# Layer 1's diagonal blocks in ten of 16 tiles, six turned on VectorE, and a quarter of the moves on ACT's queue

## The chip, the cores and the metric

The kernel runs on one core of a Trainium2 chip. A core has four compute engines that matter here: TensorE (PE, matmuls and 128x128 transposes), VectorE (DVE), ScalarE (ACT) and GpSimd (POOL). SyncE (SP) computes nothing and issues DMAs; ACT and POOL can issue them as well. Each engine runs its own list of instructions in order, and engines wait for one another on semaphores. Operands lie in the on-chip memory SBUF (128 partitions); matmuls write to PSUM. The metric is the device time of the core in microseconds, as a median over runs.

## The reference, cut to what matters

The input x is (4, 128, 64, 64): four batches, C = 128 channels, N = 4096 tokens. Everything is f32. Two layers follow one another, then a recurrent scan:

```python
# layer 0: group norm, then attention with q and k of 64 channels, gated, projected, residual
x = x + conv_attention(group_norm(x))
# layer 1
t = tokens(x)                                   # (4, 4096, 128)
h = layer_norm(t)
q = einsum('bsd,de->bse', h, W)
scores = einsum('bsd,btd->bst', q, q)           # symmetric in s and t
t = t + einsum('bst,btd->bsd', softmax(scores), h)
# FFN: batch norm over all tokens, then a scan over the 4096 tokens of each batch
wx = batch_norm(layer_norm(t) @ Wf.T)
y_t = sigmoid(wx_t + y_{t-1} @ V.T)
t = t + y
```

The point for this change is layer 1: its queries are also its keys, so the matrix of scores is symmetric, and so is its elementwise exponential. The tile for (queries s, keys t) is the transpose of the tile for (queries t, keys s).

## The kernel before, in words

**Tiling.** Of each batch, layer 1 takes the 4096 tokens as NB = 8 blocks of QB = 512 columns, and each block as NQ = 4 tiles of P = 128. A block pair (n, a) means the 512 queries of block n against the 512 keys of block a: 16 tiles of 128x128. The loop at the end of `layer1` runs over n in the order 6, 7, 5, 4, 3, 2, 1, 0 and, within each, over a from n down to 0 (`order`; the last batch's n = 0 is the exception). Because of the symmetry only pairs with a <= n are computed: one pair serves block n's output with its tiles as they are, and block a's output with its tiles turned.

**A pair takes two steps, i = 0 and i = 1.** In each, TensorE computes the scores of two key tiles against 512 queries into one of two PSUM buffers `ps` (line 726), ACT takes their exponential into `e`, one of four buffers (L730), and, if `turns(n, a)` holds (a < n, except for the last batch's pair (1, 0)), VectorE transposes the 32x32 squares of `e` into `dd`, one of two buffers (line 733). Transposing within 32x32 squares leaves the squares in the wrong partitions. So after the second step SP issues 16 DMAs of 64 KB each, from 32 partitions of `dd` to 32 partitions of `tt`, one of three buffers (lines 758 to 763, the DMA itself L760). They stay within SBUF.

**The products.** `direct` (lines 602 to 611) multiplies `e` by h of block a into the PSUM tile `o` of block n, two matmuls over 512 columns for each step, two steps later (LAG). `reversed_products` (lines 613 to 623) multiplies the turned tiles in `tt` by h of block n for block a, four matmuls, when the step count `clock` has gone on by 4 since the moves were issued. VectorE adds the finished `o` into `oacc` (`part`). When a block has all its parts, `finish` loads its tokens `t` with an SP DMA (line 655) and puts `tokens`, `turn` and `inputs` on the list `pending`, from which each step takes one. They normalize the block, write the turned result with four SP DMAs (line 279), and compute the FFN's input `wx`, which SP writes out (line 697). If `pending` is empty, a step takes a piece from `ahead`, the next batch's layer-0 inputs.

**The diagonal pair (a = n)** is not turned into `dd`. Its step i = 0 is like any other: scores over 2 x 512 columns. Its step i = 1 is `quarter` (lines 573 to 592): two matmuls over 256 columns for the lower right quarter (L578), four 128x128 transposes on TensorE that turn two tiles of each of the two key tiles of the first step's `e` (L584), an exp over 512 columns and a copy of 512 columns on ACT (L588 and L592). The products of a diagonal pair are the four 512-column matmuls of `direct`.

**Order.** At the start of the program the order of instructions is written by hand; after that (line 797) the framework's scheduler lays out each engine's list from the program as written, and the tile pools decide which buffer each allocation gets. In the built program every DMA of a queue signals one of eight completion counters, taken in turn, so that an issue waits until the DMA eight before it has landed. Layer 0 (line 461), the loads of the next batch's x, and, just before the last batch's layer 1, three SP loads of 2 MB each for `wxs` (line 820, the FFN's inputs of the batches already done) stand on the same SP queue as layer 1's moves.

## Time and profile before

| what | value |
|---|---|
| median of 3 runs | 3046.68 us (3046.57 to 3047.66) |
| the profiled execution's own time | 3047.56 us |
| its span in the trace | 3045.7 us |
| granted TensorE clock, mean | 0.994 |
| layer 1, as it stands in the trace | four stretches, one for each batch, of some 365 to 400 us |
| VectorE's transposes of squares (L733), 128x512 | 281.7 us in x444, 682 ns mean |
| exp of a step of layer 1 (L730), 128x1024 | 1.11 us mean, x258 |
| scores of layer 1 (L726), 128x512 | 482.9 us in x1032 records |
| direct products (L605), 128x512 | 537.0 us in x1160 records |

The page gives busy times of each engine, the span in 40 slices, the DMA queues, the chain of work that ended last, and groups of instructions by line, operation and shape. Two things are needed to read it. A matmul's record overlaps the one after it, because matmuls are pipelined, so the mean of a group is not the time at which the next one can begin; the pitch between successive ones is read from the chain in order of time. And an f32 matmul stands as two records, so counts of matmul records are twice the counts in the code (transposes have one).

The engines' rows in the 40 slices show where layer 1 lies: in its slices VectorE stands at 3 to 5 tenths, against 6 elsewhere, and 85 GB/s and more are moved, while TensorE stands at 9 in nearly all slices of the span.

### The profile page before, as it was taken

The numbers are of one execution on the slowest core, as the hardware profiler recorded it, in microseconds if no ns is written. First come the engines' busy times: TensorE is split into PE (matmuls) and PEld (weight loads), VectorE is DVE, ScalarE is ACT, GpSimd is POOL, SyncE is SP. The second block draws the span as 40 slices with busy tenths as digits, with TensorE's granted clock in tenths as the row PEclk, the third lists the DMA queues.
The fourth block names the chain that finished last, engine by engine and source line by source line (L and its number), as shares of the span: only waits on it lengthen the run. The fifth ranks groups of instructions, "written<-read, shape, count | busy, mean of one in ns | idle before, by whom it ended". The sixth has DMA issues, their size and how long they took to land.

```text
span 3045.7 us, 31528 instructions
## 1 busy us (share of the span) xinstructions
PE 2989.5 (98%) x10720; PEld 1371.1 (45%) x10720; DVE 1677.2 (55%) x3114; ACT 1032.2 (34%) x1151; POOL 221.0 (7%) x215
## 2 busy tenths in 40 slices
PE   9999999999999999999999999999999999999985
PEld 4444444444444444444444444444444444444442
DVE  6666654434666664444466665443456666333356
ACT  3444432222344432222244443222234443222224
POOL 0011100000011110000011101000001111000000
PEclk9999999999999999999999999999999999999998
DMA  1112143434122123333311114343422113544333
GB/s 42 41 53 56 52 117 87 97 90 99 41 56 56 48 85 96 94 96 87 87 46 56 42 47 118 85 98 87 101 58 59 39 49 90 143 100 102 96 119 151
DMA packets 246986, 241.09 MB, mean 79 GB/s; under 512 B 90016, under 2 KB 162208, under 8 KB 245792
## 3 DMA queue, kind: packets, MB, share of 16 engines
q1 hardware_dynamic: 246816, 238.98, 29.6%
q8 instruction: 88, 1.44, 0.2%
q14 instruction: 82, 0.67, 0.1%
HBM read 65.80 MB, written 56.62 MB: 40 GB/s over the span
## 4 chain that ended last, share of the span: by engine, by line
PE 92%; DVE 3%; SPq 2%; ACT 1%; DMA 0%; issue 0%; POOL 0%; DVEq 0%; POOLq 0%; ACTq 0%
PE o L476 28%; PE o L605 15%; PE ps L238 14%; PE ps L726 14%; PE ot L618 12%; SPq L760 2%; PE m L267 1%; PE m L689 1%; PE mp L438 1%; PE ps L578 1%; PE mq L570 1%; PE mp L369 1%; PE mp L423 1%; DVE t2s L900 1%; DVE ps_r L873 1%; PE m L680 1%
## 5 line engine op out<-in xcount | busy, mean ns | idle before, releaser
L476 PE MATMUL o<-e,nxt 64*128 64x512 f32 x4096 | 973.1, 589 | 0.0
L240 ACT ACTIVATE e<-ps 128x1024 f32<-128x1024 f32 x512 | 520.9, 1023 | 687.1 <-PE ps L238 648.1
L247 DVE TENSOR_TENSOR acc<-acc,e 128x1024 f32<-128x1024 f32 x448 | 547.6, 1222 | 228.5 <-ACT e L240 212.4
L476 PEld LDWEIGHTS o<-e,nxt 64*128 64x128 f32 x4096 | 403.4, 187 | 482.9 <-issue 474.1
L238 PE MATMUL ps<-nxt 64*128 64x512 f32 x2048 | 541.6, 595 | 1.9 <-ACT e L592 0.8
L605 PE MATMUL o<-e,h 128*128 128x512 f32 x1160 | 537.0, 592 | 0.0
L730 ACT ACTIVATE e<-ps,shift 128x1024 f32<-128x1024 f32 x258 | 287.2, 1113 | 646.3 <-PE ps L726 357.9
L726 PE MATMUL ps<-qt 128*128 128x512 f32 x1032 | 482.9, 594 | 2.7 <-ACT qt L571 2.7
L618 PE MATMUL ot<-tt,h 128*128 128x512 f32 x888 | 400.9, 593 | 0.0
L733 DVE STREAM_TRANSPOSE dd<-e 128x512 f32<-128x512 f32 x444 | 281.7, 682 | 137.9 <-ACT e L730 83.7
L605 PEld LDWEIGHTS o<-e,h 128*128 128x128 f32 x1160 | 218.8, 190 | 268.2 <-issue 268.0
L238 PEld LDWEIGHTS ps<-nxt 64*128 64x128 f32 x2048 | 197.9, 187 | 231.0 <-issue 148.8
L726 PEld LDWEIGHTS ps<-qt 128*128 128x128 f32 x1032 | 189.9, 190 | 219.3 <-issue 190.8
L618 PEld LDWEIGHTS ot<-tt,h 128*128 128x128 f32 x888 | 167.8, 190 | 210.2 <-issue 205.3
L627 DVE TENSOR_TENSOR oacc<-oacc,ot 128x512 f32<-128x512 f32 x87 | 59.7, 687 | 288.4 <-PE ot L618 288.4
L145 POOL TENSOR_SCALAR rstd<-mv 128x4 f32<-128x4 f32 x64 | 14.5, 226 | 2374.9 <-DVE mv L300 2374.9
L532 DVE SCALAR_TENSOR_TENSOR t<-yt,rinv,t 128x128 f32<-128x128 f32 x128 | 36.5, 347 | 80.2 <-DMA yt<-turn_d 80.2
L493 POOL TENSOR_SCALAR xb<-xb,bpc 128x512 f32<-128x512 f32 x32 | 61.6, 1924 | 243.9 <-DMA xb<-in_x_dram 234.3
L543 POOL TENSOR_SCALAR h<-h 128x512 f32<-128x512 f32 x32 | 72.3, 2261 | 63.7 <-DVE d L275 61.7
L588 ACT ACTIVATE e<-ps,shift 128x512 f32<-128x512 f32 x32 | 22.0, 687 | 144.1 <-PE ps L584 133.8
L146 POOL TENSOR_TENSOR rstd<-rstd,mhalf 128x4 f32<-128x4 f32 x64 | 66.4, 1037 | 5.3
L629 DVE COPY oacc<-ot 128x512 f32<-128x512 f32 x24 | 16.6, 691 | 85.6 <-PE ot L618 85.5
(156 smaller groups left out, 1611.2 us busy)
## 6 DMA issues: line engine op xcount, KB each, us to landing
tt<-dd SPq DMA_DIRECT2D x1776, 64.0 KB, 2.0
turn_d<-d SPq DMA_DIRECT2D x384, 64.0 KB, 1.8
nxt<-in_x_dram SPq DMA_DIRECT2D x16, 512.0 KB, 5.6
xb<-in_x_dram SPq DMA_DIRECT2D x32, 256.0 KB, 3.3
t<-turn_d SPq DMA_DIRECT2D x32, 256.0 KB, 2.7
yt<-turn_d SPq DMA_DIRECT2D x32, 256.0 KB, 2.7
t_d<-t SPq DMA_DIRECT2D x32, 256.0 KB, 2.0
qt<-turn_d SPq DMA_DIRECT2D x32, 256.0 KB, 2.9
```

Source lines behind the costliest of these rows:

```text
L146: nc.gpsimd.tensor_tensor(dst, dst, mhalf[:, :n], ALU.pow)
L238: nc.tensor.matmul(ps[:, h, :], lhsT=lhsT, rhs=rhs, start=True, stop=True)
L240: nc.scalar.activation(e, ps, AF.Exp, scale=scale)
L247: nc.vector.tensor_tensor(acc, acc, e, ALU.add)
L476: nc.tensor.matmul(o[r], lhsT=v[rs, p + h * PAIRS, :], rhs=e[rs, h, :], start=(p == 0 and h == 0), stop=(p == PAIRS - 1 and h == 1),)
L493: biased = nc.gpsimd.tensor_scalar(xb, xb, bpc, None, ALU.add)
L543: nc.gpsimd.tensor_scalar(hn, hn, 1.0, None, ALU.add)
L605: nc.tensor.matmul(o, lhsT=h[:, NQ * a + 2 * i + half, :], rhs=e[:, half, :], start=(a == order(n)[0] and i == 0 and half == 0), stop=(a = ...
L618: nc.tensor.matmul(ot, lhsT=h[:, NQ * n + j, :], rhs=t[:, :, j, :, :].rearrange("q p k j -> q k p j"), start=(j == 0), stop=(j == NQ - 1),)
L726: nc.tensor.matmul(ps[:, half, :], lhsT=qt[:, bass.ts(at, P)], rhs=qt[:, bass.ts(n, QB)], start=True, stop=True,)
L730: nc.scalar.activation(e, ps, AF.Exp, bias=shift)
L733: nc.vector.transpose(d.rearrange("q f b k j -> q k b f j")[:, 2 * i + half], e[:, half, :].rearrange("q (b f j) -> q b f j", b=NQ, f=NQ),)
```

## The change

A new function `upper(n, a)` holds for the diagonal pair of blocks n = 2 to 7, which is six pairs in each batch and 24 in all. For them only the tiles on and above the diagonal are computed, ten of 16: the scores of key tile j cover the columns from j x 128 on. In step i = 0 these are 512 and 384 columns, packed into 896 columns of `ps` and `e`; in step i = 1 256 and 128, packed into 384. Exp runs over the packed columns. `direct` multiplies just these columns.

The six tiles above the diagonal are turned by VectorE (`turn_tiles`, three transposes of 128, 256 and 256 columns in step 0, one of 128 in step 1) into a packed `dd` and moved to `tt` by 16 DMAs of 24 KB. `own_products` multiplies them into the same `o` with three matmuls over 384, 256 and 128 columns, due three steps after the moves are issued. `quarter` stays for the diagonal pairs of n = 1 and n = 0.

All moves are now issued in two parts, by `send`. The squares f = 0, 1, 2, 12 DMAs, go out on SP's queue as before. The squares f = 3, four DMAs, are put on a list `unsent`, and ACT's queue issues them after the exp of the following step. This holds for the 111 pairs that were turned before and the 24 that now are. So SP issues 1620 moves in place of 1776, and ACT 540. The tiles `dd` and `tt` keep their size, 2 and 3 buffers of 2048 columns, and are laid out flat.

The core of the diff:

```diff
@@ -554,9 +554,12 @@
             oacc = big.tile([P, NB, QB], F32, tag="oacc", name="oacc")
-            dd = big.tile([P, 2, NQ, NQ, NQ, 32], F32, tag="dd", name="dd")
-            tt = big.tile([P, 3, NQ, NQ, NQ, 32], F32, tag="tt", name="tt")
+            dd = big.tile([P, 2, NQ * QB], F32, tag="dd", name="dd")
+            tt = big.tile([P, 3, NQ * QB], F32, tag="tt", name="tt")
             fifo: deque = deque()
+            own_turned: deque = deque()
+            unsent: deque = deque()
             turned: deque = deque()
             clock = 0
             n_turned = 0
@@ -599,11 +602,75 @@
             def turns(n, a):
                 return a < n and not (b == B - 1 and n == 1)
+            def upper(n, a):
+                return a == n > 1
+            STEPS = [[slice(0, 512), slice(512, 896)], [slice(0, 256), slice(256, 384)]]
+            def columns(n, a, i, half, e):
+                if upper(n, a):
+                    j = 2 * i + half
+                    return slice(j * P, QB), e.rearrange("p a b -> p (a b)")[:, STEPS[i][half]]
+                return slice(0, QB), e[:, half, :]
+            def packed(d, n, a):
+                if upper(n, a):
+                    return d[:, : 4 * 6 * 32].rearrange("q (f s j) -> q f s j", f=4, s=6)
+                return d.rearrange("q (f b k j) -> q f b k j", f=4, b=NQ, k=NQ)
+            def turn_tiles(n, a, i, e, d):
+                if upper(n, a):
+                    flat_e = e.rearrange("p a b -> p (a b)")
+                    for at, s in (
+                        ((slice(128, 256), slice(0, 1)), (slice(256, 512), slice(1, 4, 2)),
+                         (slice(640, 896), slice(2, 5, 2)))
+                        if i == 0 else ((slice(128, 256), slice(5, 6)),)
+                    ):
+                        nc.vector.transpose(
+                            d.rearrange("q f s j -> q s f j")[:, s],
+                            flat_e[:, at].rearrange("q (s f j) -> q s f j", f=4, j=32),
+                        )
+                elif turns(n, a):
+                    for half in range(2):
+                        nc.vector.transpose(
+                            d.rearrange("q f b k j -> q k b f j")[:, 2 * i + half],
+                            e[:, half, :].rearrange("q (b f j) -> q b f j", b=NQ, f=NQ),
+                        )
+            def send(n, a, d, t, queue, fs):
+                size = (6 if upper(n, a) else 16) * 32
+                for p in range(4):
+                    for f in fs:
+                        queue.dma_start(
+                            t[bass.ts(f, 32), bass.ts(p, size)], d[bass.ts(p, 32), bass.ts(f, size)]
+                        )
+            def own_products():
+                _, n, t, o = own_turned.popleft()
+                assert fifo and fifo[-1][0] == n
+                t = t[:, : 4 * 6 * 32].rearrange("q (p s k) -> q p s k", p=4, s=6)
+                for j, s in ((3, 3), (2, 1), (1, 0)):
+                    nc.tensor.matmul(
+                        o[:, : j * P], lhsT=h[:, NQ * n + j, :],
+                        rhs=t[:, :, s : s + j, :].rearrange("q p k j -> q k p j"),
+                        start=False, stop=False,
+                    )
             def direct():
                 n, a, i, e, o = fifo.popleft()
                 for half in range(2):
+                    cols, es = columns(n, a, i, half, e)
                     nc.tensor.matmul(
-                        o, lhsT=h[:, NQ * a + 2 * i + half, :], rhs=e[:, half, :],
+                        o[:, cols], lhsT=h[:, NQ * a + 2 * i + half, :], rhs=es,
                         start=(a == order(n)[0] and i == 0 and half == 0),
                         stop=(a == order(n)[-1] and i == 1 and half == 1),
                     )
@@ -617,7 +684,7 @@
                 for j in range(NQ):
                     nc.tensor.matmul(
                         ot, lhsT=h[:, NQ * n + j, :],
-                        rhs=t[:, :, j, :, :].rearrange("q p k j -> q k p j"),
+                        rhs=t.rearrange("q (p b k j) -> q b k p j", p=4, b=NQ, k=NQ)[:, j],
                         start=(j == 0), stop=(j == NQ - 1),
                     )
                 part(a, ot)
@@ -711,29 +778,34 @@
                 if n == NB - 2:
                     queries(n)
                 for a in order(n):
-                    if turns(n, a):
+                    if turns(n, a) or upper(n, a):
                         d = dd[:, n_turned % 2]
                         t = tt[:, n_turned % 3]
                         n_turned += 1
                     for i in range(2):
                         ps = ps_s.tile([P, 2, QB], F32, tag="s", name="ps")
                         e = ep.tile([P, 2, QB], F32, tag="e", name="e")
-                        if a == n and i == 1:
+                        if a == n < 2 and i == 1:
                             quarter(n, ps, e, before)
                         else:
+                            width = 0
                             for half in range(2):
                                 at = NQ * a + 2 * i + half
+                                cols, scores = columns(n, a, i, half, ps)
                                 nc.tensor.matmul(
-                                    ps[:, half, :], lhsT=qt[:, bass.ts(at, P)],
-                                    rhs=qt[:, bass.ts(n, QB)], start=True, stop=True,
+                                    scores, lhsT=qt[:, bass.ts(at, P)],
+                                    rhs=qt[:, n * QB + cols.start : n * QB + cols.stop],
+                                    start=True, stop=True,
                                 )
-                            nc.scalar.activation(e, ps, AF.Exp, bias=shift)
-                            for half in range(2):
-                                if turns(n, a):
-                                    nc.vector.transpose(
-                                        d.rearrange("q f b k j -> q k b f j")[:, 2 * i + half],
-                                        e[:, half, :].rearrange("q (b f j) -> q b f j", b=NQ, f=NQ),
-                                    )
+                                width += cols.stop - cols.start
+                            nc.scalar.activation(
+                                e.rearrange("p a b -> p (a b)")[:, :width],
+                                ps.rearrange("p a b -> p (a b)")[:, :width], AF.Exp, bias=shift,
+                            )
+                            if turns(n, a) or upper(n, a):
+                                turn_tiles(n, a, i, e, packed(d, n, a))
+                        if unsent:
+                            unsent.popleft()()
                         before = e
                         if o is None:
                             o = ps_o.tile([P, QB], F32, tag="o", name="o")
@@ -748,19 +820,23 @@
                             direct()
                             if a == order(n)[0] and i == 0:
                                 direct()
+                        if own_turned and own_turned[0][0] <= clock:
+                            own_products()
                         if turned and turned[0][0] <= clock:
                             reversed_products()
                         if pending:
                             pending.popleft()()
                         elif ahead:
                             ahead.popleft()()
-                    if turns(n, a):
-                        for p in range(NQ):
-                            for f in range(NQ):
-                                nc.sync.dma_start(
-                                    t[bass.ts(f, 32), p], d[bass.ts(p, 32), f]
-                                )
+                    if turns(n, a) or upper(n, a):
+                        send(n, a, d, t, nc.sync, range(3))
+                        unsent.append(partial(send, n, a, d, t, nc.scalar, (3,)))
+                    if upper(n, a):
+                        own_turned.append((clock + 3, n, t, o))
+                    elif turns(n, a):
                         turned.append((clock + 4, n, a, t))
+            while unsent:
+                unsent.popleft()()
             while fifo:
                 direct()
             pending.extend([reversed_products] * len(turned))
```

## The prediction

> **What bounds the kernel now.** I read the page's busy times first, then the stretches by stage, then the chain of waits cut to layer 1, then the groups by shape, and last the SP queue. The page's busy line, followed by the busy times in the four stretches of layer 1 (columns: stretch, length, busy us of each engine with its instructions, granted clock, DMA share, GB/s):
>
> ```profile
> PE 2989.5 (98%) x10720; PEld 1371.1 (45%) x10720; DVE 1677.2 (55%) x3114; ACT 1032.2 (34%) x1151; POOL 221.0 (7%) x215
> ...
> 390.00:790.00 400.00, 398.34 (x1086) 183.85 (x1086) 183.89 (x393) 111.45 (x125) 12.42 (x19) 1.00 0.39 95
> 1120.00:1520.00 400.00, 398.34 (x1086) 183.99 (x1084) 183.69 (x392) 111.91 (x126) 12.42 (x19) 1.00 0.39 96
> 1850.00:2250.00 400.00, 398.34 (x1086) 184.26 (x1086) 183.56 (x392) 112.43 (x126) 12.42 (x19) 1.00 0.39 96
> 2580.00:2945.00 365.00, 363.20 (x931) 166.15 (x929) 139.63 (x323) 90.81 (x97) 11.61 (x17) 1.00 0.42 109
> ```
>
> In layer 1 TensorE is without work for 1565.0 - 1558.2 = 6.8 us in all four batches together. So time is won there only by giving TensorE less to do, and any wait put on TensorE is lost one to one. The price of a matmul is its pitch, not the mean in the group table, which overlaps its neighbours. The chain of waits in order of time, start and length, "x" counting records (two for each f32 matmul, one for a transpose):
>
> ```profile
> 539.93 0.89 PE mp L423 x8
> ...
> 545.98 0.86 PE ps L578 x4
> 546.84 0.57 PE m L660 x4
> 547.41 0.44 PE ps L584 x4
> 547.85 3.44 PE ps L726 x8
> 551.28 3.43 PE ot L618 x8
> ```
>
> A matmul over 512 columns costs 3.43/4 = 0.858 us, over 256 columns 0.86/2 = 0.43, over 128 columns 0.89/4 = 0.223, a 128x128 transpose 0.11. That is 1.68 us per 1000 columns almost without a floor: the 128-wide matmuls, whose weights change as often, are only 4% dearer per column. For 384 columns no row exists; I take 0.643 on that line.
>
> The second resource is the SP queue, which issues every move of the turned tiles:
>
> ```profile
> L760 SPq DMA_DIRECT2D tt<-dd x1776: 507/589/1965, 399.7 to 2917.5; - x198
> ...
> 682.69 10.01 SPq L760 DMA_DIRECT2D tt<-dd  x16
> ...
> 2578.51 10.15 SPq L820 DMA_DIRECT2D wxs<-wxs_d  x3
> 2593.66 2.68 SPq L279 DMA_DIRECT2D turn_d<-d  x4
> 2596.38 1.86 SPq L760 DMA_DIRECT2D tt<-dd  x3
> ...
> DMA to landing us min/median/max: 10.3/15.7/19.4
> ```
>
> Sixteen moves take 10.0 us, 0.63 each, and a block pair gives TensorE 12 x 0.858 = 10.3 us. SP is nearly as full as TensorE, but TensorE waits only 2.7 us for moves in the whole run (the tile view of tt). The last lines are the start of the last batch: three 2 MB loads (landing times in the last line) hold SP for 10 us, and the first moves go out at 2596.
>
> **What the Trainium skill says.** "DMA: Bandwidth & Descriptors", section "Issuing engines are not separate DMA queues": several issuing engines share the same 16 DMA engines and save only the sequencer's time of issue. The trace fits: a move lands 2.0 us after issue (median) while SP is busy 0.589 us for each, so issue is what is scarce. The same page, "Queues, rings and completion order", adds that SP and ACT have a ring of their own on each DMA engine but no descriptor generator of their own; no ACT issue stands in this trace, so whether two queues really issue twice as fast isn't shown. "TensorE: Matmul & The Clock Gate", section on the 16x 32x32 array: ACT's queue is strictly first in, first out, while TensorE can pull weight loads ahead. The second half agrees: the loads of 0.19 us sit beside the running matmuls, at 256 columns too. The first half means that an exp stands behind any move ACT has to wait for.
>
> **The change, part by part.** TensorE, diagonal block with n > 1 (six for each batch, 24 in all). Removed: scores 2 x 0.858 + 2 x 0.43 = 2.58, four transposes 0.44, products 4 x 0.858 = 3.43; sum 6.45 us. Added: scores over 512, 384, 256 and 128 columns, 0.858 + 0.643 + 0.43 + 0.223 = 2.15; the direct products over the same columns 2.15; the three products with turned tiles (384, 256, 128) 1.30; sum 5.61 us. Saved 0.84 us each, 24 x 0.84 = 20.2 us. All of it is on TensorE's path.
>
> VectorE: four transposes of 128, 256, 256 and 128 columns per block. By width from the 512-wide row of L733 (682 ns) they are 768/512 x 0.68 = 1.0 us; at the 340 ns of VectorE's 128x128 rows (another operation) each, 1.4; some 24 to 34 us beside an engine 46% busy in layer 1. Counted at nothing; it is hidden by the 5.6 us of TensorE's diagonal block.
>
> ACT: exp shrinks from 1024 + 512 columns and a 0.58 us copy to 896 + 384. It gains 540 moves, four for each block pair. Their cost on ACT isn't in the trace: bounds 0.4 us (the large loads on SP) and 0.8; I take SP's 0.63, 2.5 us for a pair. With two exps of 1.11 that fills 4.7 of 10.3 us. The next scores but one need the exp of the step, because there are two score buffers: TensorE has other products and one pair of scores in between, at least 5 us. So four moves fit if ACT doesn't stand waiting.
>
> SP: 12 moves for each of 135 pairs, 1620 instead of 1776. A pair costs 7.6 us against 10.3 us of TensorE; a diagonal one 7.6 against 5.6, paid back by the next pair. SP stops being full after the first blocks of a batch.
>
> Added waits: in the built program the DMAs of both queues take eight completion counters in turn, so an issue waits for the eighth DMA before it, whichever queue that is on. Behind ACT's moves stand the next exps, behind SP's the t loads, the turned results and wx. I followed three places by hand with the durations above.
> First, an ordinary block start: between the diagonal scores and its turned products (due three steps on) stand some 16 us of TensorE work; SP needs what is left of the pair before, 12 issues and 2 us to land. The margin is 7 us for block 7 and 4.4 us for block 2, where ACT's four moves take counters ahead of SP's first and cost it 1.5 us.
> Second, the start of batches 0 to 2: SP's first move waits for the 512 KB loads of the next x (from 387 to 391 us in batch 0); twelve issues end at 398.8, land at 400.8; TensorE's own work from its first projection at 384.7 adds up to 17.4 us and reaches the turned products at about 402. Margin 1 us, no wait.
> Third, the start of the last batch: the third 2 MB load now waits for the counter of a move before it and for the first load's landing (2578.5 + 10.3), and the sixth move of the diagonal block waits for the third load's counter, which by bandwidth (350 GB/s in that stretch) lands near 2601 as before. Seven more issues, 4 us, and 2 us to land: 2607. TensorE, 2576.3 + 26.6 us of work placed ahead, arrives at 2603. It waits 4 us. Bounds: nothing, if the loads land sooner; 9 us, if ACT's moves are held in the same jam.
>
> Sum: -20.2 + 4.1 = -16 us. The profiled execution ends 1.9 us above its span (3047.6 against 3045.7) and 0.9 above the median; span 3045.7 becomes 3029.6, and from the median of 3046.7 I get 3030.6, say **3031**.
>
> **Rivals.** *No wait at all:* the loads land in time and the moves fit. Then 3046.7 - 20.2 = 3026.5, or up to 2.7 us less if the old waits for moves go too, 3024. For it: SP is relieved. Against: that the load comes ahead of the moves in SP's order.
> *Turned products come late at every block:* if the two queues don't issue side by side, a move of 16 takes 10 us again and each diagonal move arrives 2 x 2.5 = 5 us later than I placed it, against margins of 1 to 7 us. At about half a us for each of the 24, 12 us: 3043, the gain eaten. For it: the missing generator of its own. Against: SP's 0.43 us for a 512 KB load against 0.59 for a 64 KB move looks like a cost of the instruction, not of data.
> *Slower: ACT held by SP's counters.* Place: the first block of each batch, where SP also carries the tail of layer 0 (8 turned pieces, two reads, one write) and stands waiting for VectorE. ACT's fourth move waits for SP's fifth; if SP is a whole move behind, ACT stands 7.6 us in a pair with 10.3 - 4.7 = 5.6 us to spare, and exp and TensorE are 2 us late. 28 such pairs cost 56 us: 3031 + 56 = 3087. It turns the sign from 0.6 us per pair. For it: SP ran without a gap from 439.6 to 520 us. Against: it has a quarter less to issue there.
>
> **How the numbers follow.** Forecast 0.70 (own range 3026 to 3037), no wait 0.12, late products 0.09 (half of it inside 0.2%), ACT held 0.09. A change below 0.2%, 6 us, can't be told from none here. Faster 0.70 + 0.12 + 0.04 = 0.86, same 0.05, slower 0.09. The range runs from 3024 (no wait, old waits gone) to 3042, near the late products, and leaves out the slower case and a little more.
>
> **What would show it.** Right: 24 diagonal blocks of 5.6 us in the chain; TensorE idle in layer 1 still under 2 us in each of the first three batches; one wait of TensorE for tt, about 4 us, near 2603; SP with gaps where it ran through; ACT issues of about 0.63 us. Wrong: ACT's exp waiting on moves, ACT issues above 1 us, a wait before most groups of turned products, or narrow matmuls with a pitch above 0.25 us.

## The result and the profile after

The changed kernel takes 3024.07 us in the median (3022.84 to 3025.18), against 3046.62 us before in the same comparison: a ratio of 0.9926, with a 95% interval of 0.9914 to 0.9938, or 22.6 us less. Forecast were 3031 us and 16 us less. The profiled execution's span went from 3045.7 to 3021.6 us.

First the page's busy line of the changed kernel:

```profile
PE 2963.2 (98%) x10768; PEld 1381.4 (46%) x10768; DVE 1718.1 (57%) x3210; ACT 1017.0 (34%) x1127; POOL 217.5 (7%) x215
```

TensorE's busy time fell by 26.3 us. Then the busy times in the four stretches that hold its layer 1 (columns as before: stretch, length, busy us of PE, PEld, DVE, ACT and POOL with instructions, granted clock, DMA share, GB/s):

```profile
385.00:785.00 400.00, 398.70 (x1128) 189.74 (x1128) 197.69 (x420) 111.67 (x124) 12.42 (x19) 1.00 0.41 102
1105.00:1505.00 400.00, 397.51 (x1121) 189.02 (x1119) 197.04 (x420) 110.96 (x123) 12.42 (x19) 1.00 0.41 102
1830.00:2230.00 400.00, 398.86 (x1129) 189.93 (x1129) 197.76 (x421) 111.72 (x123) 12.42 (x19) 1.00 0.41 102
2550.00:2920.00 370.00, 363.92 (x948) 170.69 (x946) 149.11 (x347) 87.75 (x93) 11.60 (x17) 0.99 0.44 114
```

TensorE is idle for 1.1 to 2.5 us in each of the first three stretches, and for 6.1 us in the last; before, it was 1.7 us in each of the first three and 1.8 in the last. The next view, the chain in order of time, shows one diagonal block (n = 4 of batch 0) with its pieces between other work:

```profile
542.25 1.51 PE ps L795 x4
...
547.18 0.65 PE ps L795 x4
...
554.44 1.50 PE o L672 x4
...
557.66 0.65 PE o L672 x4
...
565.18 1.30 PE o L662 x6
```

Their sum is 5.61 us, where the old block took 6.45. The third view is the waits of TensorE (waiting tile and line, what it waited for, us in all, times, longest):

```profile
PE o L662 <- DMA tt<-dd: 3.6, 3, 3.1
...
PE o L662 <- issue: 1.5, 1, 1.5
...
PE ps L795 <- ACT e L801: 1.3, 4, 0.4
```

The new products (L662) wait four times, 5.1 us together, 3.1 of it once ("issue" is idle time for which the profile shows no cause). Layer 1's exp makes TensorE wait 1.3 us in the whole run.

To see where the time went, each batch is measured from one landmark to the next: the start of the last unbroken group of layer-0 products (5.15 us long, L476 x24 in the chain), just ahead of layer 1. The first two of these landmarks before, then with the change:

```profile
379.65 5.15 PE o L476 x24
...
1110.16 5.15 PE o L476 x24
```

```profile
379.38 5.15 PE o L476 x24
...
1101.01 5.15 PE o L476 x24
```

Batch 3 with the scan runs to the end of the span.

| us | batch 0 | batch 1 | batch 2 | batch 3 and scan | span |
|---|---|---|---|---|---|
| before | 730.51 | 730.52 | 730.51 | 474.51 | 3045.7 |
| the change | 721.63 | 722.70 | 721.44 | 476.45 | 3021.6 |
| split alone | 725.98 | 725.98 | 725.99 | 477.62 | 3034.8 |
| split alone, loads later | 725.99 | 725.97 | 725.98 | 476.81 | 3034.5 |
| the change, loads later | 721.75 | 722.45 | 721.32 | 469.90 | 3014.8 |
| the change, all moves on SP | 737.91 | 741.04 | 739.81 | 512.82 | 3111.0 |

Six diagonal blocks save 6 x 0.84 = 5.0 us for each batch. Batches 0 to 2 gained 7.8 to 9.1, so 3 to 4 us each came from elsewhere; batch 3 lost 1.9 where it should have gained 5.0, so some 7 us went missing there. Both need an explanation.

### The profile page after: what moved, and what is told of

It is laid out like the page before. It is cut to its first block, busy times and chain, and to the rows that moved or that the text cites. A ratio compares the mean times of both kernels' runs of the same rounds, so it can differ in the third digit from the quotient of the medians.

```text
span 3021.6 us, 32547 instructions
## 1 busy us (share of the span) xinstructions
PE 2963.2 (98%) x10768; PEld 1381.4 (46%) x10768; DVE 1718.1 (57%) x3210; ACT 1017.0 (34%) x1127; POOL 217.5 (7%) x215
## 3 DMA queue, kind: packets, MB, share of 16 engines
q1 hardware_dynamic: 239328, 216.95, 26.6%
## 4 chain that ended last, share of the span: by engine, by line
PE 94%; DVE 2%; DMA 2%; ACT 1%; SPq 1%; issue 0%; POOL 0%; DVEq 0%; ACTq 0%; POOLq 0%
PE o L476 29%; PE o L672 15%; PE ps L238 15%; PE ps L795 14%; PE ot L685 13%; PE o L662 1%; PE m L756 1%; PE m L267 1%; PE mp L369 1%; PE mp L438 1%; DMA tt<-dd 1%; DMA wxs<-wxs_d 1%; PE mp L423 1%; DVE t2s L976 1%; DVE ps_r L949 1%; SPq L652 1%
## 5 line engine op out<-in xcount | busy, mean ns | idle before, releaser
L476 PE MATMUL o<-e,nxt 64*128 64x512 f32 x4096 | 966.5, 589 | 0.0
L476 PEld LDWEIGHTS o<-e,nxt 64*128 64x128 f32 x4096 | 400.5, 187 | 482.6 <-issue 473.8
L801 ACT ACTIVATE e<-ps,shift 128x1024 f32<-128x1024 f32 (+2 forms) x282 | 298.4, 1059 | 730.4 <-PE ps L795 417.0
L238 PE MATMUL ps<-nxt 64*128 64x512 f32 x2048 | 533.3, 595 | 1.2 <-ACT e L240 0.6
L672 PE MATMUL o<-e,h 128*128 128x512 f32 (+3 forms) x1160 | 511.0, 567 | 0.0
L795 PE MATMUL ps<-qt 128*128 128x512 f32 (+3 forms) x1128 | 502.0, 567 | 4.0 <-ACT qt L574 2.7
L795 PEld LDWEIGHTS ps<-qt 128*128 128x128 f32 x1128 | 208.3, 190 | 229.8 <-issue 207.9
L381 ACT ACTIVATE nxt<-mp,par 64x512 f32<-64x512 f32 x31 | 23.9, 772 | 115.7 <-DVE nxt L377 99.8
L303 DVE TENSOR_SCALAR h<-t,mv,rstd 128x128 f32<-128x128 f32 x128 | 35.7, 343 | 46.8 <-POOL rstd L146 46.8
```

Source lines behind the costliest of these rows:

```text
L238: nc.tensor.matmul(ps[:, h, :], lhsT=lhsT, rhs=rhs, start=True, stop=True)
L476: nc.tensor.matmul(o[r], lhsT=v[rs, p + h * PAIRS, :], rhs=e[rs, h, :], start=(p == 0 and h == 0), stop=(p == PAIRS - 1 and h == 1),)
L672: nc.tensor.matmul(o[:, cols], lhsT=h[:, NQ * a + 2 * i + half, :], rhs=es, start=(a == order(n)[0] and i == 0 and half == 0), stop=(a == ...
L795: nc.tensor.matmul(scores, lhsT=qt[:, bass.ts(at, P)], rhs=qt[:, n * QB + cols.start : n * QB + cols.stop], start=True, stop=True,)
L801: nc.scalar.activation(e.rearrange("p a b -> p (a b)")[:, :width], ps.rearrange("p a b -> p (a b)")[:, :width], AF.Exp, bias=shift,)
```

## The experiments

Ten more kernels were run, each timed beside the kernel before on the same chip. They come in the order of the questions.

### Is it the smaller blocks, or the second queue?

Two kernels take the change apart. The first keeps the ten-tile blocks and puts all moves back on SP:

```diff
-                        send(n, a, d, t, nc.sync, range(3))
-                        unsent.append(partial(send, n, a, d, t, nc.scalar, (3,)))
+                        send(n, a, d, t, nc.sync, range(4))
```

> The changed kernel with all 16 moves of a pair on SP's queue, none on ACT's; the diagonal blocks as in the change. Theory A (the gain is TensorE's smaller diagonal blocks plus a better order at the hand-over to layer 0, and ACT's share of the moves only keeps the turned tiles in time): 24 x 0.84 = 20.2 us and the hand-over stay, but the moves of a diagonal block end 2.5 us later (four more issues of 0.63 us), at the four batch starts with nothing to spare and at other blocks beyond their margin too: some 10 to 18 us of new waits of TensorE for tt, 3034 to 3042 us. Theory B (the gain comes from taking a quarter of the moves off a full SP queue): the gain is gone, 3044 to 3050 us. If the ACT queue does nothing for TensorE: 3024 us.

The second is the kernel before with only the split of the moves:

```diff
-                        for p in range(NQ):
-                            for f in range(NQ):
-                                nc.sync.dma_start(
-                                    t[bass.ts(f, 32), p], d[bass.ts(p, 32), f]
-                                )
+                        send(d, t, nc.sync, range(3))
+                        unsent.append(partial(send, d, t, nc.scalar, (3,)))
```

> The kernel before with its own diagonal blocks (quarter for all n), only the moves split: 12 on SP, four on ACT a step later. Theory A: the waits for moves go, at most 2.7 us, and so do the hand-over's lone layer-0 matmuls that the order of before has (three scores instead of two or four ahead of a full-array group, in three batches), some 2.7 us for each of three batches: 3046.6 - 2.7 - 8.2 = 3036 us (3033 to 3040). Theory B (relief of SP is the gain): 3024 to 3030 us. Theory C (the hand-over gains nothing by itself, and the extra 3.8 us for each batch belong to the diagonal blocks): 3044 us.

The ten-tile blocks alone took **3112.99 us**, 66 us more than before (ratio 1.0221, interval 1.0207 to 1.0235); no theory had that. The split alone took **3035.47 us** (ratio 0.9961, 0.9948 to 0.9975), 11.4 us less than before, as theory A had it. The change against the split alone is another 11.4 us. So the two halves aren't independent: the blocks are worth something only when SP has been relieved, and relieving SP is worth something without them.

The page's shares of the chain that ended last, for the first kernel (SPq is SP's queue of issues):

```profile
PE 82%; SPq 11%; DVE 3%; DMA 1%; issue 1%; ACT 1%; POOL 0%; DVEq 0%; ACTq 0%; POOLq 0%
```

A piece of its chain in order of time, from the last batch:

```profile
2917.52 0.59 SPq L652
2918.16 0.59 SPq L652
2918.79 0.59 SPq L652
2919.42 1.81 DMA tt<-dd
2921.33 2.90 PE o L662 x6
```

The chain runs through SP for 11% of the span, in unbroken rows of issues 0.63 us apart, then through the landing of the last move, and only then through the products that waited. In the changed kernel SP has 1%. The size of a move doesn't help: a 24 KB move of a diagonal block costs SP the same 0.59 us and 0.04 us of gap as a 64 KB one. So a diagonal block asks SP for 16 x 0.63 = 10.1 us while giving TensorE 5.6 us of work, and the pairs after it, 10.1 against 10.3, pay nothing back. The prediction wrote "paid back by the next pair" of 7.6 against 10.3, which holds with 12 moves and not with 16.

Waits are not the whole loss. Against the change, TensorE is idle for 53 us more and busy for 36 us more (2999.5 against 2963.2) with the same work. Part of the busy time is the clock: in layer 1 it stands at one half in ten stretches, 41 us together, and in the change in one, 6.8 us.

A further kernel asked whether it is SP's total that counts or the diagonal block's own lateness. Only the 24 diagonal blocks are split:

```diff
-                        send(n, a, d, t, nc.sync, range(3))
-                        unsent.append(partial(send, n, a, d, t, nc.scalar, (3,)))
+                        send(n, a, d, t, nc.sync, range(3 if upper(n, a) else 4))
+                        if upper(n, a):
+                            unsent.append(partial(send, n, a, d, t, nc.scalar, (3,)))
```

> The changed kernel with only the 24 diagonal blocks' moves split 12 and 4; the other 111 pairs send all 16 on SP, as before. SP then issues 1776 + 288 = 2064 moves, against 2160 with everything on SP (3113 us), 1620 in the change and 1776 before. Theory A (SP's total number of issues is what decides: with 2160 moves of 0.63 us it has no gap in layer 1 and TensorE follows it): most of the loss stays, 3075 to 3105 us. Rival (only the diagonal block's own moves come too late with 16 on one queue): 3024 to 3032 us.

It took **3090.09 us** (ratio 1.0136, 1.0121 to 1.0152), as theory A had it: taking 96 issues off SP brought back 23 of the 89 us between the change and all moves on SP. So most of the cost is not the diagonal block's own 16 moves but SP's total: TensorE waits 12.4 us ahead of the own products and 11.4 us ahead of the other pairs' turned products. From 1620 moves on SP at 3024 us the time goes to 3090 at 2064 and 3113 at 2160.

### Does it matter that the second queue is ACT's?

The split alone again, with the four moves on GpSimd's queue:

```diff
-                        unsent.append(partial(send, d, t, nc.scalar, (3,)))
+                        unsent.append(partial(send, d, t, nc.gpsimd, (3,)))
```

> As the split alone (before's diagonal blocks, 12 moves on SP), but the four moves of a pair go out on GpSimd's queue a step later, not ACT's. Theory A (what counts is that SP has a quarter less to issue; which second queue takes it doesn't matter as long as it is idle): within 3 us of the split alone, 3033 to 3038 us. Rival (it is ACT's queue, with its exps between the moves, that gives the order and the time): 3044 us and more, or GpSimd's issues take far longer than 0.6 us each and the moves come late: above 3050 us.

**3035.01 us** (0.9962, 0.9948 to 0.9975): the same as with ACT. The moves' lines in the view of tile tt, first of the split with ACT, then with GpSimd (issuing line and engine, count, ns least/median/most, first and last start):

```profile
L607 SPq DMA_DIRECT2D tt<-dd x1332: 507/589/3072, 399.3 to 2897.1; - x191
...
L607 ACTq DMA_DIRECT2D tt<-dd x444: 514/601/847, 399.3 to 2891.8; - x148
```

```profile
L607 POOL DMA_DIRECT2D tt<-dd x444: 496/496/719, 400.5 to 2892.7; - x148
```

An issue takes 0.60 us on ACT and 0.50 on GpSimd. This is what the Trainium skill, "Perfetto Trace Analysis", section "DMA Optimizations", advises where the generation of descriptors is the limit rather than the transfer: to balance DMAs over the engines that can issue them. The runs agree: 11.4 us less with four of 16 moves on ACT, 12.1 with four on GpSimd.

One thing this pair of runs can't decide. Put in order of their start, 2559 of TensorE's 10720 records stand for another operation with the split than before, though only moves were edited; between the splits with ACT and with GpSimd not one differs. So a relieved SP and a new order of TensorE's work came together, in both.

The opposite way was tried too: no second queue, but more patience. In the kernel before, the turned products come due five steps after their moves in place of four:

```diff
-                        turned.append((clock + 4, n, a, t))
+                        turned.append((clock + 5, n, a, t))
```

> The kernel before, whole, all moves on SP and no ten-tile blocks; only the turned products of a pair are due five steps after their moves in place of four, which also gives the built program another order at the hand-over from layer 1 to layer 0, without the odd groups of three layer-0 scores. Theory A (the 11 us of the split alone are the end of TensorE's waits for moves and of the lone layer-0 matmuls, and come from order and slack, not from ACT's queue as such): 3034 to 3038 us, 4 to 4.5 us less in each of the first three batches, with lone layer-0 matmuls gone from the trace. Rival (the second queue itself is what gives those 11 us): 3044 to 3047 us.

**3062.78 us** (1.0049, 1.0035 to 1.0063), slower by 16 us; both theories missed it. TensorE hardly waits for moves there, but each batch is 3 to 5 us longer. A good part of that is a wait for VectorE's normalized rows of finished blocks, 3.0 us against 0.5 in each of the first three batches. From the waits of TensorE, before and with this kernel:

```profile
PE m L680 <- DVE h L303: 1.9, 4, 0.5
```

```profile
PE m L680 <- DVE h L303: 11.7, 8, 1.7
```

What sets the order in this kernel wasn't followed further. This one step of slack doesn't do what the second queue does.

### Where do the split's 4.5 us for each batch come from?

In the first three batches the split alone gains 4.52 to 4.54 us. TensorE's idle time explains 1.7 us of it for each batch (2.34 us before, 0.68 with the split): 0.8 is a wait just before a layer-0 projection, for moves in two of the batches, and the rest lies in the hand-over from layer 1 to layer 0. Before:

```profile
PE mp L369 <- DMA tt<-dd: 1.7, 2, 0.8
```

The other 2.9 us are time in which TensorE was busy. Compare the hand-over in TensorE's timeline. First before (start, us, line, tiles, shapes, records, idle time ahead in brackets):

```profile
757.66 1.13 PE L238 MATMUL ps<-nxt 64*128 64x512 f32 x4
759.05 1.12 PE L238 MATMUL ps<-nxt 64*128 64x512 f32 x2 [0.25 <-ACT e L592]
760.10 3.70 PE L618 MATMUL ot<-tt,h 128*128 128x512 f32 x8
...
769.95 0.59 PE L476 MATMUL o<-e,nxt 64*128 64x512 f32 x1
770.37 0.59 PE L238 MATMUL ps<-nxt 64*128 64x512 f32 x1
770.38 1.87 PE L476 MATMUL o<-e,nxt 64*128 64x512 f32 x6
...
778.36 1.10 PE L680 MATMUL m<-ident,h 128*128 128x128 f32 x4 [0.53 <-DVE h L303]
```

Then the same place with the split alone:

```profile
763.42 1.13 PE L238 MATMUL ps<-nxt 64*128 64x512 f32 x4
764.48 0.66 PE L667 MATMUL m<-ident,oacc 128*128 128x128 f32 x4
765.07 1.99 PE L238 MATMUL ps<-nxt 64*128 64x512 f32 x8
766.89 1.88 PE L476 MATMUL o<-e,nxt 64*128 64x512 f32 x8
768.61 1.02 PE L238 MATMUL ps<-nxt 64*128 64x512 f32 x4
769.47 1.88 PE L476 MATMUL o<-e,nxt 64*128 64x512 f32 x8
```

Layer 0's matmuls use 64 rows each and go in pairs: with the split, x4 (two matmuls of two records) take 0.86 us from start to start (768.61 to the next group), 0.215 for each record. A record alone, x1 at 769.95 before, takes 0.42. The Trainium skill says why ("TensorE: Matmul & The Clock Gate", "Part 3: Packing small matmuls — row/col tiling"): matmuls that would leave part of the array idle can be placed on different tiles of it and then run at the same time. In the order of before, three scores stand ahead of a full-array group, not two or four. The third (x2 at 759.05) fills 1.05 us to the next start instead of 0.43, and until the next odd group the timeline shows records in ones where they should run in twos. The first six score records, 1.29 us of work in step, take 2.44 with 0.25 us of waiting, and from 768.98 to 777.83 38 records take 8.85 us instead of 8.15; with the wait of 0.53 it is 2.4 us, against 0.5 with the split. Neither the change nor the split alone has such odd groups in layer 1's hand-over. So the hand-over gives 1.9 us and the wait ahead of the projections 0.8. The rest, about 1.8 us for each batch, is busy time and isn't split up further. That this order follows from SP's relief fits both split kernels, but wasn't shown apart from it.

In its last batch the split alone is 3.1 us longer than before. Of this, 2.3 us are waits for VectorE's normalized rows of the last blocks (L303: 1.8 and 5.9 us, against 0.3 and 5.1).

### What did the last batch lose?

TensorE's timeline at the start of the changed kernel's last layer 1, and its clock there (stretch, length, busy us, clock, DMA share, GB/s):

```profile
2577.46 1.13 PE L573 MATMUL mq<-qt,w 128*128 128x512 f32 x2 [0.67 <-ACT qt L574]
2581.69 2.90 PE L662 MATMUL o<-tt,h 128*128 128x384 f32 x6 [3.10 <-DMA tt<-dd]
2584.38 8.25 PE L672 MATMUL o<-e,h 128*128 128x512 f32 x16
2592.47 1.88 PE L795 MATMUL ps<-qt 128*128 128x512 f32 x4
```

```profile
2577.00:2582.00 5.00, 1.44 (x3) 0.80 0.22 56
2582.00:2586.00 4.00, 4.00 (x8) 0.50 0.44 110
2586.00:2590.00 4.00, 4.00 (x10) 0.90 0.68 197
2590.00:2594.00 4.00, 4.00 (x11) 1.00 0.44 131
```

The own products wait 3.10 us. After that they take 2.69 us from start to start instead of 1.30, and the next 16 records 8.09 instead of 6.87: another 2.6 us, because the clock is granted at one half. The Trainium skill has it: "TensorE: Matmul & The Clock Gate", Part 1, "What's actually happening", says that the array falls to half clock after an idle window of about 3.4 us. The trace agrees on the half clock, but not on so long an idle time: windows of half a us show 1.00 up to 2580.0 and 0.50 after it, 1.4 us after TensorE had stopped at 2578.6. With the 0.67 us ahead this is 6.4 of the 7 us that were missing.

Two kernels tested the cause. In one the three loads are written later, behind the moves of other pairs:

```diff
-                for i in range(B - 1):
-                    nc.sync.dma_start(wxs[:, :, i, :, :], wxs_d[i])
...
+                    if b == B - 1 and (n, a) in ((5, 3), (4, 2), (3, 1)):
+                        nc.sync.dma_start(wxs[:, :, 5 - n, :, :], wxs_d[5 - n])
```

> The changed kernel with the three 2 MB loads of wxs taken from the start of the last batch's layer 1 and issued on the same queue later, one each after the moves of the pairs (5, 3), (4, 2) and (3, 1). Theory A (the loads hold SP's moves of the last batch's first diagonal block, TensorE waits 3.1 us for them and then runs at half clock for some 4 us): the wait and the 2.6 us of slow matmuls go, 3024 - 5.7 = 3018 us, and the last batch saves about 5 us against before where it now loses 2. Rival (the moves are late there because SP carries the tail of layer 0, whatever the loads do): 3023 to 3024 us. A rival on the other side (the loads now hold the moves of the blocks beside them): 3026 to 3035 us.

**3020.66 us**, 3.4 less than the change where 5.7 were expected. In the built program only two of the loads moved. From SP's timeline, first the change, then this kernel:

```profile
2552.47 10.06 SPq L896 DMA_DIRECT2D wxs<-wxs_d  x3
```

```profile
2552.19 0.60 SPq L835 DMA_DIRECT2D wxs<-wxs_d  x1
```

That let the first block's moves begin at 2556.0 in place of 2563.1. The wait fell to 1.39 us and the clock stayed full. But two new waits for moves came up later in the batch, 1.1 and 1.6 us, after the loads' new places. In the other kernel the loads stay, and the products of each batch's first block come later:

```diff
-                        own_turned.append((clock + 3, n, t, o))
+                        own_turned.append((clock + (5 if n == NB - 2 else 3), n, t, o))
```

> The changed kernel with the products of the first diagonal block of each batch (n = 6) due five steps after its moves in place of three. Theory A (the four waits before these products, 0.4, 1.5, 0.5 and 3.1 us, and the half clock after the last, 2.6 us, are the whole price of moving these tiles): all go, 3024 - 8 = 3016 us. Rival (the wait moves on to the next group of turned products, since SP is behind as a whole there): 3021 to 3024 us.

**3021.71 us**, 2.4 less, where 8 were expected. That is inside the rival's range, but the wait did not move on to the next turned products: 1.78 us of it stayed with the own products, again at full clock. In batches 0 and 2 the kernel lost half a us each instead of gaining, beside new waits of 2.9 us, in three places, for ACT's copy of qt. Both kernels say the same of the last batch: once the wait is below 2 us, the half clock is gone too, and that was the larger part of what they gained.

Put together, with the loads written after the pairs (7, 6), (7, 3) and (5, 4), and one more step for the last batch's first block:

```diff
+            LOADS = [(7, 6), (7, 3), (5, 4)]
...
+                    if b == B - 1 and (n, a) in LOADS:
+                        i = LOADS.index((n, a))
+                        nc.sync.dma_start(wxs[:, :, i, :, :], wxs_d[i])
...
+                        own_turned.append((clock + (4 if b == B - 1 and n == NB - 2 else 3), n, t, o))
```

> The changed kernel with the wxs loads issued later, after the moves of the pairs (7, 6), (7, 3) and (5, 4), each at least three pairs ahead of a diagonal block, and the first diagonal block's own products of the last batch due four steps after their moves in place of three. Theory A: the last batch's waits for moves go (1.4, 1.1 and 1.6 us where the loads were only put later), 3020.7 - 4 = 3016 to 3017 us, and the last batch takes some 469 to 470 us from its last layer-0 products to the end. Rival (each 2 MB load holds up the moves wherever it stands): 3020 to 3024 us.

**3018.50 us** (3016.56 to 3019.43; ratio 0.9907, 0.9892 to 0.9922), the fastest of all, and between its two theories. Again one load stays at the start (2552.22); the others are issued at 2672.34 and 2726.04. TensorE's waits for the own products' moves:

```profile
PE o L663 <- DMA tt<-dd: 1.4, 3, 1.0
```

The last batch takes 469.90 us, 6.6 less than in the change; the trace is of the fastest of its runs. To read from it what the blocks are worth alone, the split of before got the same loads:

```diff
+            LOADS = [(7, 6), (7, 3), (5, 4)]
...
                         send(d, t, nc.sync, range(3))
+                        if b == B - 1 and (n, a) in LOADS:
+                            i = LOADS.index((n, a))
+                            nc.sync.dma_start(wxs[:, :, i, :, :], wxs_d[i])
```

> The kernel before with its own diagonal blocks, the moves split 12 on SP and four on ACT, and the wxs loads issued later, after the moves of the pairs (7, 6), (7, 3) and (5, 4). Beside the changed kernel with the same loads (3018.5 us) it differs only in the diagonal blocks and in one due time. Theory A (in the split kernel without ten-tile blocks nothing waits for the loads, since its first turned products come some 20 us later than the ten-tile block's own products): within 2 us of the split alone, 3034 to 3036 us, so that the diagonal blocks alone are worth 16 to 18 us once nothing waits. Rival (the last batch's 3 us that the split alone lost against before come from the loads): 3031 to 3033 us.

**3035.20 us**, where the split alone took 3035.47, as theory A had it. In the built program only one of the three loads moved (two are issued from 2565.01 on, one at 2638.80), so the run alone says little of their place; but TensorE waits for no move in the last batch of either kernel. The blocks alone, with little left to wait for, are worth 3035.20 - 3018.50 = 16.7 us in the medians. The two traces are 3034.5 - 3014.8 = 19.7 us apart, but one is of a run above its kernel's median and the other of a run below.

### How much can ACT's queue carry?

The change with eight of a pair's 16 moves on each queue:

```diff
-                        send(n, a, d, t, nc.sync, range(3))
-                        unsent.append(partial(send, n, a, d, t, nc.scalar, (3,)))
+                        send(n, a, d, t, nc.sync, range(2))
+                        unsent.append(partial(send, n, a, d, t, nc.scalar, (2, 3)))
```

> The changed kernel with the moves halved between the queues: eight on SP, eight on ACT a step later. Theory A (a quarter already takes SP off the path; what TensorE still waits for is the last batch's loads and the batch starts): within 3 us of the change, 3021 to 3027 us, TensorE's waits for exp below 5 us in all. Rival (SP's issue is still the limit): 3016 to 3019 us. Rival on the other side (ACT's eight issues, 4.8 us, and two exps, 2.2 us, with the waits of its issues for counters no longer fit in a pair, so exps come late): above 3030 us, with TensorE's scores waiting for exp.

**3030.78 us** (0.9947, 0.9934 to 0.9961), 6.7 more than the change. That is at the edge of the range in which ACT is too full (above 3030), though TensorE waits only 2.6 us for exp; it waits 8.8 us for ACT's copies of qt, against 3.4 in the change. In the spans 4.4 of 7.5 us are in the last batch, again at its start (TensorE's timeline):

```profile
2567.90 1.98 PE L795 MATMUL ps<-qt 128*128 128x512 f32 x4 [1.08 <-ACT e L801]
...
2576.31 3.32 PE L795 MATMUL ps<-qt 128*128 128x512 f32 x4 [2.13 <-ACT qt L574]
...
2586.40 2.27 PE L662 MATMUL o<-tt,h 128*128 128x384 f32 x6 [2.12 <-DMA tt<-dd]
```

With eight moves on it, ACT stands in the jam of the loads at the start of the last batch, and its exp and its copy of qt come late. In the change, with four, it also stands for long, and nothing comes of it. From the view of tile tt of the change:

```profile
L652 ACTq DMA_DIRECT2D tt<-dd x540: 514/601/1388, 390.5 to 2880.4; - x180
...
  ACT e L801: 244.5, 53
```

The second line is under "who waited": ACT's exps are held 244.5 us in 53 places by moves ahead of them, and TensorE waits 1.3 us for exp in all.

## Why the prediction was right, and where it was off

The sign held, and the diagonal blocks did what the sum said of them. That the time lies in the range is partly luck. 3024.07 us is at its very edge (3024), outside the forecast's own 3026 to 3037, and on the figure of the rival in which nothing waits, though TensorE did wait. The sum was some 7 us off because two terms were mis-sized, and these partly cancelled: the split of the moves was worth 11.4 us in place of nothing, and the waits cost some 9 us (20.2 + 11.4 - 22.6) in place of 4.1; 8.4 of it can be read off, 6.4 in the last batch and 2.0 ahead of the first own products of the other three.

- *Diagonal blocks, 0.84 us each, 20.2 us.* Right: 5.61 us for the block shown in the chain, and 16.7 us in the medians (19.7 in the traces) of two kernels that differ besides only in one due time and in which loads stand at the start of the last batch. The assumed 384-wide pitch of 0.643 is 1.51 - 0.86 = 0.65. Narrow matmuls stayed on the line.
- *VectorE at nothing.* Right. Its four transposes take 0.31, 0.40, 0.40 and 0.31 us, 1.4 in all, the upper of the two estimates, and the view of tile tt puts 0.5 us of idle time in the whole run to VectorE's turned tiles.
- *ACT's issue at 0.63 us, and the queues side by side.* Right: 0.60 us, and GpSimd's 0.50. The rival of late products, in which two queues give no more than one, fell. It was also priced far too low: at 12 us, where the kernel with one queue for everything loses 66 against before and 89 against the change. The step that failed in it is "half a us for each of the 24": lateness doesn't stay with its block once SP has no gap in which to catch up.
- *SP "stops being full", counted at nothing but the 2.7 us of old waits, and that only in a rival.* This is the term that failed. The split alone gives 11.4 us. SP did stop being full: before, 126 moves run unbroken for 93.18 us from 429.46 on, where in the change SP stands still for 3.6 us ahead of 505. TensorE's idle time showed little of the gain, since 2.9 of the 4.5 us for each batch were lost inside TensorE's busy time, in matmuls out of step and in smaller pieces. Whether it is SP's relief that gives the time, or the new order of TensorE's work that came with it, stays open. And the 2.7 us are misread: they are idle time of the weight loads. TensorE itself waited 1.7 us for moves, in two places.
- *No wait at ordinary block starts and in batches 0 to 2, margins of 1 to 7 us.* Nearly: the margin of 1 us was too small for its working, and the own products wait 0.24, 1.52 and 0.26 us at the start of those batches.
- *One wait at the start of the last batch, 4.1 us.* Right in place and cause, and nearly in size: 3.1 us. The forecast was 26.6 us after layer 1's start for TensorE and 4 later for the moves; TensorE stopped 28.4 us after it. What was missing is the price of a wait: the half clock behind it cost 2.6 us more.
- *Slower, with ACT held by SP's counters.* ACT was held, and more than thought (244.5 us), but the two score buffers and the products in between covered it. The run with eight moves on ACT shows where that cover ends. Exps that wait on moves were named as a sign of being wrong; they came, and the sum held, because an exp's wait costs only where TensorE then waits for the exp.

## What to carry to other kernels

When a change adds work to a queue that is nearly full, price the queue's total over the stage, not the lateness of the added items: here 384 more issues on SP turned a saving of 20 us, as the sum has it, into a loss of 66. A second issuing queue took a quarter of the issues and cost TensorE 1.3 us of waiting for exp; without the new blocks, it made no difference whether it was ACT's or GpSimd's. The scheduler answers an edit of the moves with another order of everything, so look in the trace where instructions really stand: of three loads written later, one or two stayed where they were. A busy engine can still be losing time to the order of its work, so look at the pitch of its matmuls as well as at its idle time.

## What the runs showed of the hardware that wasn't expected

A move of 24 KB costs the issuing queue as much as one of 64 KB, 0.59 us on SP. While ACT issues four moves in 2.44 us (at 560.24 and again at 579.79 in the change), SP issues four in 2.71 and three in 2.48: the queues work side by side, with SP at 0.68 to 0.83 us for each in place of 0.63. And TensorE's clock fell to half after less idle time than the page cited above names: in the change 1.4 us into a wait (with 0.67 us of idle time a little ahead of it), and in the kernel with half of the moves on ACT after 2.13 us (the four records behind it took 3.32 us in place of 1.88). A bound doesn't come out of these runs: waits of 1.39 and 1.78 us left the clock at full, but behind a wait of 1.67 us in the kernel with the later due time it stood at 0.50, and two records took 1.70 us in place of 0.86. Once down, it stayed there for 3.4 us or twice that in layer 1 of every kernel in which it fell.
